# Two banks of an early convolution, and a gate, inside the last Mamba chunk's scan

## The chip, the cores and the metric

The kernel runs on one core of one Trainium2 chip. The metric is the device time of one execution in microseconds (us). A core has five instruction queues that run beside one another and wait for each other through semaphores: TensorE (PE: matmuls, with its weight loads shown apart as PEld), VectorE (DVE), ScalarE (ACT), GpSimd (POOL), and SyncE (SP), which here only starts DMA transfers. Each queue runs its instructions in the order in which they stand.

## What is computed

The reference is a network of four layers on an input of 2 x 256 x 32 x 32, all in float32. Only the first two matter here.

```python
# layer 0: two Mamba blocks, tokens = 1024 per image, 512 inner channels, 16 states
xr = u @ in_w + in_b;  xs, res = jnp.split(xr, 2, axis=-1)
xs = silu(causal_conv4(xs));  delta = softplus(dt @ dt_w + dt_b)
hst = exp(delta * A) * hst + delta * Bm * xs        # per state, a recurrence over tokens
y = einsum('bdn,bn->bd', hst, C) + xs * Dp
out = (y * silu(res)) @ out_w + out_b               # then layernorm, and added to the input
# layer 1: a dilated 7 x 7 convolution to 128 channels, a 1 x 1 convolution to 49 logits per
# pixel, a softmax over them, and with it a weighted sum of the 49 shifted images
k = conv(conv(x, w1, dilation=2, padding=6) + b1, w2) + b2;  attn = softmax(k, axis=1)
x = einsum('bkchw,bkhw->bchw', shifts, attn)
...
```

`silu(res)` is the gate. Layers 2 and 3 (linear attention, softmax attention, two mixtures of experts) take the second half of the time and are the same in both kernels.

## The kernel before, in words

**Chunks.** Layer 0 (`layer0`, L575) works on 2,048 tokens in four chunks of 512 for each of two blocks, eight units in all. `front` (L293) makes a chunk's inputs, `scan` (L415) runs the recurrence, `back` (L485) turns its sum into the chunk's result and adds it to `x`.

**The scan.** For each of 16 states, a DMA on SP brings a row of B to all partitions; POOL multiplies it with `du` (L461, two products of 128 x 1024 into `h`, six buffers, which are three states); ACT makes the decay (L468, four times, into PSUM buffers `da`); DVE runs the recurrence (L472, four scans of 128 x 512). The generator `rest` (L434) then turns the state's result: four times, PE transposes four 128 x 128 blocks into a PSUM tile `ht` (L440, three buffers), and DVE adds the tile, scaled, to `ya` (L449). For states 0 and 10 ACT does that (L447).

**PSUM.** It holds eight banks. In the last unit they are two for `da` (`m_da2`, L634), one for the convolution (`m_acc`, L635), two for `mm` and three for `ht`.

**The early convolution.** Layer 1's two convolutions are folded into one set of weights in advance (`taps`). `Taps.convolve` (L748) computes the logits of one image into up to three PSUM banks of 16 rows x 32 columns. Its 56 steps are four weight groups u (3, 0, 1, 2) by seven taps by two halves of the channels; a step issues one matmul for each bank that it was given and that the tap reaches:

```python
for k, a in acc.items():
    lo, hi = max(16 * k, r0), min(16 * k + 16, r0 + W)
    if lo < hi:
        nc.tensor.matmul(a[:, lo - 16 * k : hi - 16 * k, co : co + n], lhsT=lhsT, ...)   # L762
    yield
```

Bank 0 is reached over 16, 10, 12 and 14 rows by the four groups, bank 1 over 16 rows by each, and bank 2 over 6, 4 and 2 rows by the last three; a tap's width is 32, 26, 28, 30, 30, 28 or 26 columns. So bank 0 has 56 matmuls over 20,800 columns, bank 1 56 over 25,600, bank 2 42 over 4,800. A float32 matmul leaves two records in the trace; a transpose leaves one. `Taps.read` (L770) copies a finished bank to `lg`: half of it by ACT (L781), then half by DVE (L779). The weights lie in `early_3`, `early_0`, `early_1`, `early_2`, loaded by SP (L740) into buffers that earlier chunks have left free.

**The order.** `scan` has 63 slots, one after each recurrence on DVE but the first; `paced` (L552) spreads side work over them by (steps, how many, first slot, last slot). In the last unit that is the ninth to sixteenth step of the previous chunk's `back`, and bank 0 of the first image in slots 3 to 63. After the scan, the last transposes are issued, and `both` (L566) issues three steps of the convolution of banks 1 and 2 to one step of the last chunk's `back`. The program's order is a priority: when the instructions are placed, one that has no buffer yet lets later ones pass, so the order on each engine differs from the listing.

**`back` by steps.** Four gate groups (PE L494, two matmuls; ACT L498) and one Silu over all (L502); four `y` (PE L507, L512; DVE L516 multiplies by the gate); four `out` (PE L524, L528); the normalization (DVE L160 to L166, ACT L150, L168); two times four transposes (L179), ACT L540, and POOL's two additions to `x` (L543, L548).

**Layer 1.** It loads the same weights again as `pair` (memset by POOL, L737, DMA by SP, L740) into memory that `early` held, transposes image 0 for the weighted sum (`xk`: copies by POOL L856, PE L857, ACT L861), and convolves the second image (`acc`, L762), whose last 512 tokens are what the last chunk's `back` writes.

Of the kernel before, what the change touches and what calls it, by code (L numbers as in the profile page):

```python
# [10 lines left out]
F32 = mybir.dt.float32  # L11
# [8 lines left out]
P = 128  # L20
# [7 lines left out]
TC = 512  # L28
# [523 lines left out]
def paced(n, parts):  # L552

    taken = [0] * len(parts)
    for slot in range(n):
        for i, (steps, many, first, end) in enumerate(parts):
            while taken[i] < many and slot >= first + (end - first) * taken[i] / many:
                next(steps, None)
                taken[i] += 1
        yield  # L560
    for steps, *_ in parts:
        for _ in steps:
            pass


def both(a, b, n):  # L566

    for i, _ in enumerate(a):
        if i % n == n - 1:
            next(b, None)  # L570
    for _ in b:
        pass


def layer0(net, x, x_dram, m1, m2, load_image, taps, conv_dram, lg):  # L575

    tc, nc = net.tc, net.nc  # L580
    with (
        tc.tile_pool(name="m_w", bufs=1) as wpool,
        tc.tile_pool(name="m_one", bufs=1) as one,
        tc.tile_pool(name="m_two", bufs=2) as two,
        tc.tile_pool(name="m_scan", bufs=2) as scanp,
        tc.tile_pool(name="m_dram", bufs=2, space=DRAM) as dram,
        tc.tile_pool(name="m_mm", bufs=2, space=PSUM) as ps_mm,
        tc.tile_pool(name="m_ht", bufs=3, space=PSUM) as ps_ht,
        ExitStack() as last,
    ):  # L590
        ps_da = last.enter_context(tc.tile_pool(name="m_da", bufs=3, space=PSUM))
        xt = x.rearrange("p c b t -> p c (b t)")
        pools = (wpool, one, two, scanp, dram, ps_mm, ps_da, ps_ht)
        blocks = [
            Mamba(net, "m1", pools, xt, None, *m1), Mamba(net, "m2", pools, xt, x_dram, *m2)
        ]
        norm = GroupNorm(net, wpool, ps_ht, x)
        blocks[0].load()
        for _ in blocks[0].diagonals():
            pass  # L600
        load_image()
        for _ in blocks[0].load_rest():
            pass
        rows = net.first_rows(wpool, ["m1_out_b", "m2_out_b"])
        for m, r in zip(blocks, rows):
            m.out_b = r
        norm.image(0)
        units = [(m, j) for m in blocks for j in range(NCH)]
        norm.image(1)
        for _ in units[0][0].front(0, alone=True):  # L610
            pass
        before, done = iter(()), []
        aside = taps.make(ps_mm, conv_dram)
        for u, (m, j) in enumerate(units):
            steps = [(b, Mamba.GATED, 0, 35) for b in done]
            fronts = []
            for a, k in units[u + 1 : u + 2]:
                if k == 0:
                    a.load()
                fronts.append(a.front(k))  # L620
            if u == NCH - 2:

                steps.append((blocks[1].diagonals(), NDC * 4, 26, 38))
            rest = m.load_rest() if u and j == 0 else iter(())
            steps += [(f, Mamba.HEAD, 0, 38) for f in fronts]
            steps += [(rest, 1, 37, 38)]
            steps += [(f, 16, 38, 62) for f in fronts] + [(b, 7, 40, 61) for b in done]
            steps += [(rest, 1, 62, 63)]
            if u + 1 < len(units):
                n = 9 if u else 12  # L630
                steps += [(islice(aside, n), n, 40, 63)]
            else:
                last.close()
                m.ps_da = last.enter_context(tc.tile_pool(name="m_da2", bufs=2, space=PSUM))  # L634
                ps_acc = last.enter_context(tc.tile_pool(name="m_acc", bufs=1, space=PSUM))  # L635

                def place(u):
                    pool, tag, w = {
                        3: (one, "pre", TC + 3), 0: (two, "xs", TC), 1: (two, "delta", TC),
                        2: (two, "du", TC),  # L640
                    }[u]
                    a = pool.tile(
                        [P, NDC, w], F32, tag=tag, name=f"early_{u}",
                        bufs=3 if tag == "xs" else None,
                    )
                    return taps.load(u, a.rearrange("p d t -> p (d t)"))

                pair = {u: place(u) for u in taps.ORDER}
                acc = {0: taps.bank(ps_acc.tile([P, TC], F32, tag="acc", name="early_acc"))}
                steps += [(taps.convolve(0, pair, acc), 56, 3, 63)]  # L650
            before = m.scan(j, before, paced(63, steps), u == 0)
            done = [m.back(j)]
        taps.read(acc, lg)
        for _ in before:
            pass
        acc = {
            k: taps.bank(ps_ht.tile([P, TC], F32, tag="ht", name=f"early_acc{k}")) for k in (1, 2)
        }
        both(taps.convolve(0, pair, acc), done[0], 3)
        taps.read(acc, lg)  # L660

# [944 lines left out]
def conv_attn_hybrid(ctx: ExitStack, tc: tile.TileContext, a: dict, out: bass.AP):  # L1606
# [6 lines left out]
    with tc.tile_pool(name="conv_w", bufs=2) as convw:  # L1613
        def load_x(b):
            for cc in range(NCC):
                nc.sync.dma_start(x[:, cc, b, :], a["x"][b, cc])

        load_x(0)
        taps = Taps(net, convw, main, x, a["l1_w1"], a["l1_w2"])
        layer0(  # L1620
            net, x, a["x"],
            [a[f"m1_{k}"] for k in ("in_w", "out_w", "xproj_w", "dt_w")],
            [a[f"m2_{k}"] for k in ("in_w", "out_w", "xproj_w", "dt_w")],
            lambda: load_x(1), taps, conv_dram, lg,
        )
# [117 lines left out]
```

## Time and profile before

| what | value |
|---|---|
| time, median of 3 runs (lowest, highest) | 2186.85 us (2185.29, 2189.43) |
| the profiled execution's own time | 2188.29 us |
| its span in the trace | 2186.6 us |
| mean TensorE clock granted | 0.918 |
| busy: PE / DVE / ACT / POOL | 87% / 64% / 44% / 47% of the span |
| last chunk's first recurrence starts | 913.8 us |
| last chunk's last transposes start | 1033.7 us |
| first matmul of the second image's convolution starts | 1116.6 us |

A view of groups gives a line of the kernel, engine, operation, the tile written and the tiles read, how often, busy time, mean duration, and the idle time of the engine just before, with what ended it. The timeline gives start, length, engine and line in order of time. A view of windows gives, for a stretch of time, each engine's busy time with the number of its records in brackets, and the mean granted clock (PEclk). Matmuls are pipelined: a record's length is longer than the distance to the next, so the pace of PE is read from distances between starts.

### The profile page before, as it was taken

How to read it: one execution, taken by the hardware profiler on the slowest of the kernel's cores; microseconds unless marked ns; L12 is line 12 of the kernel's file. 1: busy time of each engine (PE TensorE's matmuls, PEld its weight loads, DVE VectorE, ACT ScalarE, POOL GpSimd, SP SyncE). 2: the span in 40 equal slices, each digit the busy share in tenths (PEclk: the TensorE clock that was granted, in tenths of full speed). 3: DMA queues.
4: the chain of work that ended last, by engine and by line, in shares of the span. 5: the costliest groups of instructions: out<-in, count | busy, mean ns of one | idle time of the engine just before them, and what ended most of it. 6: DMA issues, size and time to landing. Idle time of an engine off the chain costs nothing.

```text
span 2186.6 us, 27311 instructions
## 1 busy us (share of the span) xinstructions
PE 1894.0 (87%) x9652; PEld 1335.5 (61%) x9652; DVE 1400.3 (64%) x2210; ACT 959.2 (44%) x1610; POOL 1028.9 (47%) x726
## 2 busy tenths in 40 slices
PE   6888898898978888788999989949999599859996
PEld 2464555556555655454646556539999467649995
DVE  6999998999999999899005475752222544432223
ACT  4676677767777767645013454411111132301111
POOL 3796787959698686965025420012332000023331
PEclk9869889898989889899999999969999799979997
DMA  2121121111212111310030100028998200059997
GB/s 106 45 68 39 37 69 35 58 35 45 62 47 60 38 49 35 85 42 17 0 64 1 48 15 10 20 82 306 326 329 323 82 10 10 20 206 327 329 323 292
DMA packets 90499, 223.87 MB, mean 102 GB/s; under 512 B 35467, under 2 KB 51728, under 8 KB 79732
## 3 DMA queue, kind: packets, MB, share of 16 engines
q1 hardware_dynamic: 77636, 198.29, 27.1%
q0 software_dynamic: 7728, 19.15, 2.9%
q10 hardware_dynamic: 4992, 4.59, 0.7%
q8 instruction: 81, 1.33, 0.3%
q14 instruction: 62, 0.51, 0.1%
HBM read 204.60 MB, written 19.37 MB: 102 GB/s over the span
## 4 chain that ended last, share of the span: by engine, by line
PE 32%; DVE 22%; issue 19%; POOL 11%; ACT 10%; DMA 5%; POOLq 0%; SPq 0%; DVEq 0%; ACTq 0%
DVE m_h L472 11%; DVE m_ya L449 6%; PE acc L762 3%; POOL x L1520 3%; POOL l_yd L1570 3%; PE m_ht L440 3%; PE early_acc L762 3%; PE av L1276 3%; ACT m_da L468 2%; PE sc L1250 2%; DMA l_yd<-y,target 2%; POOL m_h L461 2%; PE h L1099 2%; PE m_xd_ps L351 1%; PE w L1108 1%
## 5 line engine op out<-in xcount | busy, mean ns | idle before, releaser
L461 POOL TENSOR_TENSOR m_h<-m_du,m_b 128x1024 f32<-128x1024 f32 x254 | 594.5, 2364 | 196.0 <-PE m_ht L440 95.8
L440 PE MATMUL m_ht<-ident,m_h 128*128 128x128 f32 x2048 | 361.2, 305 | 119.4 <-DVE m_ya L449 83.9
L440 PEld LDWEIGHTS m_ht<-ident,m_h 128*128 128x128 f32 x2048 | 259.5, 154 | 317.8 <-DVE m_ya L449 112.7
L468 ACT ACTIVATE m_da<-m_delta,m_aneg 128x512 f32<-128x512 f32 x512 | 349.5, 690 | 220.8 <-DVE m_h L472 220.1
L1520 POOL DMA_INDIRECT x<-l_zd,source x82 | 84.8, 1034 | 573.1 <-DVE source L1465 217.1
L449 DVE SCALAR_TENSOR_TENSOR m_ya<-m_ht,m_ct,m_ya 128x512 f32<-128x512 f32 x448 | 320.2, 733 | 18.4 <-PE m_ht L440 17.5
L472 DVE TENSOR_TENSOR_SCAN m_h<-m_da,m_state,m_h 128x512 f32<-128x512 f32 x256 | 318.7, 1271 | 14.7 <-POOL m_h L461 8.7
L472 DVE TENSOR_TENSOR_SCAN m_h<-m_da,m_h 128x512 f32<-128x512 f32 x256 | 303.3, 1210 | 23.6 <-ACT m_da L468 13.1
L1550 PEld LDWEIGHTS h<-xts,we 128*128 128x128 f32 x2528 | 298.4, 194 | 7.1 <-issue 3.4
L1550 PE MATMUL h<-xts,we 128*128 128x128 f32 x2528 | 299.4, 277 | 2.2 <-issue 1.7
L1557 DVE TENSOR_TENSOR hid<-hid,h 128x512 f32<-128x512 f32 x79 | 54.3, 688 | 258.9 <-PE h L1550 258.9
L1556 ACT ACTIVATE hid<-h 128x512 f32<-128x512 f32 x79 | 47.2, 598 | 384.6 <-issue 324.0
L1564 PE MATMUL o<-we,hid 128*128 128x256 f32 x632 | 150.4, 380 | 2.2 <-DVE y L1569 1.6
L1570 POOL DMA_INDIRECT l_yd<-y,target x79 | 79.3, 1003 | 142.6 <-DVE y L1569 136.3
L1564 PEld LDWEIGHTS o<-we,hid 128*128 128x128 f32 x632 | 113.7, 190 | 15.7 <-DVE y L1569 2.8
L336 PE MATMUL m_conv<-m_pre,m_taps 128*128 128x512 f32 x240 | 114.6, 596 | 6.7 <-ACT m_gate L498 5.6
L762 PE MATMUL early_acc<-x,early 128*98 128x448 f32 (+21 forms) x308 | 97.0, 447 | 0.0
L762 PE MATMUL acc<-x,pair 128*98 128x416 f32 (+21 forms) x308 | 93.6, 452 | 0.0
L1569 DVE COPY y<-o 128x256 f32<-128x256 f32 x79 | 33.6, 425 | 69.6 <-PE o L1564 69.6
L309 PE MATMUL m_in<-x,m_in_sb 128*128 128x512 f32 x128 | 68.8, 663 | 9.8 <-ACT m_pre L313 6.9
L762 PEld LDWEIGHTS acc<-x,pair 128*98 128x98 f32 x308 | 47.7, 167 | 39.9 <-issue 34.5
L528 PE MATMUL m_out<-m_out_sb,m_xs 128*128 128x256 f32 x256 | 68.7, 397 | 0.0
(318 smaller groups left out, 2843.3 us busy)
## 6 DMA issues: line engine op xcount, KB each, us to landing
we<-in_l_experts_dram SPq DMA_DIRECT2D x82, 1536.0 KB
m_b<-m_bd SPq DMA_DIRECT2D x128, 256.0 KB
w<-in_l_w_dram SPq DMA_DIRECT2D x21, 256.0 KB
l_zd<-l_z SPq DMA_DIRECT2D x7, 512.0 KB
l_yl<-l_yd SPq DMA_DIRECT2D x10, 256.0 KB
l_yl<-l_yd ACTq DMA_DIRECT2D x10, 256.0 KB
early<-taps SPq DMA_DIRECT2D x7, 343.0 KB
pair<-taps SPq DMA_DIRECT2D x7, 343.0 KB
```

The costliest lines, as they stand in the source:

```text
L309: nc.tensor.matmul(ps, lhsT=self.in_sb[:, kc, mc * P : (mc + 1) * P], rhs=self.xt[:, kc, tok], start=(kc == 0), stop=(kc == NCC - 1),)
L336: nc.tensor.matmul(ps, lhsT=self.taps[:, dc * 4 + k, :], rhs=pre[:, dc, k : k + TC], start=(k == 0), stop=(k == 3),)
L440: nc.tensor.transpose(ps[:, dc * P : (dc + 1) * P], hs[dc // G][:, dc % G, i * P : (i + 1) * P], net.ident,)
L449: nc.vector.scalar_tensor_tensor(ya[:, i, :], ps, c, ya[:, i, :], ALU.mult, ALU.add)
L461: (nc.vector if start and n == 0 else nc.gpsimd).tensor_mul(h, du[:, g * G : (g + 1) * G, :], b.unsqueeze(1).to_broadcast(half))
L468: nc.scalar.activation(da, delta[:, dc, :], AF.Exp, scale=self.aneg[:, i : i + 1])
L472: nc.vector.tensor_tensor_scan(h, da, h, 0.0 if first else state[:, n, dc : dc + 1], ALU.mult, ALU.add)
L762: nc.tensor.matmul(a[:, lo - 16 * k : hi - 16 * k, co : co + n], lhsT=lhsT, rhs=self.x[:, kc, b, lo - r0 : hi - r0, ci : ci + n], start=(u ...
L1520: nc.gpsimd.indirect_dma_start(out=x, out_offset=None, in_=zd[:, :], in_offset=bass.IndirectOffsetOnAxis(ap=source[:, g : g + 1], axis=0), ...
L1550: nc.tensor.matmul(ps[:, at], lhsT=w12[:, s, kc, at], rhs=xt[:, kc * P : (kc + 1) * P], start=(kc == 0), stop=(kc == NCC - 1),)
L1564: nc.tensor.matmul(ps[:, :C], lhsT=ht[:, mc * P : (mc + 1) * P], rhs=w[:, 8 + mc, :], start=(mc == 0), stop=(mc == NHC - 1),)
L1570: nc.gpsimd.indirect_dma_start(out=yd[g], out_offset=bass.IndirectOffsetOnAxis(ap=target[:, g : g + 1], axis=0), in_=y, in_offset=None, bo ...
```

## The change

Bank 1 of the first image follows bank 0 in the last scan, in the same PSUM bank, with a read of each when it is done; the last chunk's own gate (five steps of `back`) is placed in slots 44 to 58; after the scan only bank 2 and the other eleven steps of `back` are left. Lines below the edit move down by seven.

```diff
                 pair = {u: place(u) for u in taps.ORDER}
-                acc = {0: taps.bank(ps_acc.tile([P, TC], F32, tag="acc", name="early_acc"))}
-                steps += [(taps.convolve(0, pair, acc), 56, 3, 63)]
+                def early():
+                    for k in range(2):
+                        a = ps_acc.tile([P, TC], F32, tag="acc", name=f"early_acc{k}")
+                        acc = {k: taps.bank(a)}
+                        yield from taps.convolve(0, pair, acc)
+                        taps.read(acc, lg)
+
+                steps += [(early(), 112, 3, 63)]
+            own = m.back(j)
+            if u + 1 == len(units):
+
+                steps += [(islice(own, 5), 5, 44, 58)]
             before = m.scan(j, before, paced(63, steps), u == 0)
-            done = [m.back(j)]
-        taps.read(acc, lg)
+            done = [own]
         for _ in before:
             pass
-        acc = {
-            k: taps.bank(ps_ht.tile([P, TC], F32, tag="ht", name=f"early_acc{k}")) for k in (1, 2)
-        }
+        acc = {2: taps.bank(ps_ht.tile([P, TC], F32, tag="ht", name="early_acc2"))}
         both(taps.convolve(0, pair, acc), done[0], 3)
         taps.read(acc, lg)
```

## The prediction

> **What bounds the kernel now.** I first asked where the work that the change touches lies. The view of windows, over the last chunk's scan and what follows it (start and end in us, length, then busy time and records of PE, PEld, DVE, ACT and POOL, the clock and the DMA share):
>
> ```profile
> core 0: us, PE busy (x) PEld busy (x) DVE busy (x) ACT busy (x) POOL busy (x), PEclk, DMA share, GB/s
> ...
> 934.50:985.00 50.50, 44.20 (x242) 29.00 (x243) 50.50 (x58) 22.61 (x30) 32.88 (x15) 1.00 0.14 42
> 985.00:1034.60 49.60, 43.56 (x207) 25.13 (x206) 49.17 (x63) 27.38 (x41) 28.39 (x14) 1.00 0.06 16
> 1034.60:1060.00 25.40, 25.40 (x99) 14.21 (x98) 1.86 (x3) 5.17 (x5) 0.00 (x0) 1.00 0.00 1
> ...
> 1110.30:1116.60 6.30, 4.49 (x14) 2.17 (x15) 0.71 (x2) 2.69 (x8) 4.07 (x13) 0.73 0.97 159
> ```
>
> In the scan DVE is busy all the time. After it DVE is empty and PE is full, until 1110.3, and then neither is. So the stretch has two limits, one after the other, and moving PE's work from the second into the first can only gain as much as PE has free in the scan. How much that is, the busy column doesn't tell, since matmuls overlap; PE's own timeline does, by distances between starts:
>
> ```profile
> 949.36 0.66 PE L440 MATMUL m_ht<-ident,m_h 128*128 128x128 f32 x4
> 949.85 0.63 PE L762 MATMUL early_acc<-x,early 128*98 128x280 f32 x2
> 950.32 1.02 PE L507 MATMUL m_y<-m_xs,m_skip 128*128 128x512 f32 x2
> ...
> 953.03 0.66 PE L440 MATMUL m_ht<-ident,m_h 128*128 128x128 f32 x4 [0.73 <-DVE m_ya L449]
> ...
> 1033.72 1.04 PE L440 MATMUL m_ht<-ident,m_h 128*128 128x128 f32 x8
> 1034.59 9.50 PE L762 MATMUL early_acc<-x,early 128*98 128x512 f32 x24
> 1043.93 1.88 PE L494 MATMUL m_g<-x,m_gate_sb 128*128 128x512 f32 x4
> 1045.65 0.86 PE L762 MATMUL early_acc<-x,early 128*98 128x416 f32 x2
> ```
>
> Four transposes take 0.44 (eight from 1033.72 to 1034.59) to 0.49 us (949.36 to 949.85); I use 0.47. The 24 records at 1034.59 cover 5,568 columns twice in 9.34 us: 0.84 ns per column and record. A gate group takes 1.72 (1043.93 to 1045.65). From the same timeline, a `y` group takes 2.65 and an `out` step 2.45. At 953.03 PE stood idle because DVE had not freed an `ht` buffer: that is the scan's usual wait. DVE's pace, from its timeline, is 1.19 for a recurrence and 0.64 for an addition to `ya`, 1.83 for both:
>
> ```profile
> 988.27 1.28 DVE L472 TENSOR_TENSOR_SCAN m_h<-m_da,m_state,m_h 128x512 f32<-128x512 f32 x1
> 989.46 0.74 DVE L449 SCALAR_TENSOR_TENSOR m_ya<-m_ht,m_ct,m_ya 128x512 f32<-128x512 f32 x1
> 990.10 1.28 DVE L472 TENSOR_TENSOR_SCAN m_h<-m_da,m_state,m_h 128x512 f32<-128x512 f32 x1
> ```
>
> Last, what starts layer 1, in the timeline of POOL and PE:
>
> ```profile
> 1105.02 1.27 POOL L548 TENSOR_TENSOR x<-x,m_x 128x512 f32<-128x512 f32 x1
> ...
> 1110.26 0.68 POOL L737 MEMSET pair<- 128x686 f32 x1 [2.59 <-PE early_acc L762]
> ```
> ```profile
> 1111.42 0.41 PE L857 MATMUL xk<-ident,xs 128*128 128x128 f32 x2 [1.22 <-POOL pair L737]
> ...
> 1116.57 13.93 PE L762 MATMUL acc<-x,pair 128*98 128x512 f32 x31
> ```
>
> The last chunk was in `x` at 1106.3, but the weights' memory came free only with the last early matmul, at 1110.2; DMA and 13 `xk` transposes then took until 1116.57. That start is the point I price.
>
> **What the Trainium skill says.** "Perfetto Trace Analysis", Identifying the Most-Contended Engine: matmul busy time is a poor measure of how full PE is. The trace agrees: transposes of 273 ns each start 0.11 us apart. "TensorE: Matmul & The Clock Gate", Part 1: an idle window of about 3.4 us drops the array to half clock. It agrees: the clock is 1.00 up to 1110.3 and 0.73 in the thin 6.3 us after it. "ScalarE: Activation LUTs", What ACT_TABLE_LOAD costs: about 1,283 ns a load; the rows before and after the gate's Silu show 1283 each.
>
> **The change, part by part.** Times are those of the profiled execution (2188.29 us, span 2186.6), 1.4 above the median.
>
> *PE's work in the scan.* Both orders agree up to state 1's transposes, at 925.2. From there to the end of bank 1 PE has: the other 50 matmuls of bank 0, 18,048 columns x 2 x 0.835 ns = 30.1; bank 1, 25,600 x 2 x 0.835 = 42.8 (new); transposes of states 1 to 14, 56 x 0.47 = 26.3; the previous chunk's four `y`, 10.6, four `out`, 9.8, and last 1.5 gate groups, 2.6; its own four gates, 6.9 (three of them lay in the scan's end already); eight result transposes, 0.9. Sum 130.0, so bank 1 can't end before 1055.2, where bank 0 ended at 1023.7 and the last transposes at 1034.6. PE, not DVE, is the scan's limit now.
>
> *PE's idle time in it.* I followed the order in which the changed program's instructions stand, with the paces above. First half: by the end of bank 0 PE needs 55.7, to 980.9, and DVE, which has 24 recurrences, 21 additions and 3 gate products from 934.55 to the addition that frees the buffer for state 7's third tile, needs 43.9, to 978.5. So PE is just ahead as the limit; it waits 1.4 for state 1's recurrence, 2.1 for one buffer behind three recurrences, 0.8 for another: 4.3. POOL's product for a state needs the buffers of three states earlier, freed by PE; it is ready at the moment it is needed (979.2 for 978.5), no more.
>
> *The wait that is added.* Bank 1 uses bank 0's buffer. Its first matmul waits for both reads; DVE's stands behind 4 recurrences and 3 additions. PE has two and a half tiles of transposes to do meanwhile, and all later transposes are queued behind: 0.8 us.
>
> *The gate.* Its matmuls need `mm` buffers, which the previous chunk's `out` holds until the normalization has read it on ACT; that waits for DVE, which waits for a transpose. The second gate group so stops PE by about 2.4 us (bounds 0 and 6). On ACT the Silu and two table loads (1.91 + 2 x 1.28) now stand ahead of the last two decays; DVE has over 10 us of slack there, so I cost them at nothing; without the slack they would cost 4.5. In the tail, before, Silu lay beside the convolution: removing it gains nothing there by itself. No part that is moved issues a DMA; SP's queue keeps its order.
>
> Bank 1 ends at 1055.2 + 4.3 + 0.8 + 2.4 = 1062.7; call that E.
>
> *The tail.* DVE reads bank 1 behind ACT (1.0), then adds four tiles (2.6): E + 3.7. Four `y`, with the first half done: E + 12.2; gate product, then `out` with bank 2 between, E + 24.8; bank 2's middle, 44 records at 0.11 to 0.17 us each (no row shows it alone; I take 0.12), covers the normalization's 4.1: E + 30; transposes, E + 31.6; two ACT results, then POOL's four additions, 1.27 each, the last perhaps late for its DMA (0.8): E + 38. In the new order POOL's memset and band work (2.1) follow, then `xk`; nine transposes now precede `acc`, not 13, and take 3.3: E + 43.7 = 1106.4. The DMA (6.2 after the last early matmul, E + 33) is hidden. What is late last is POOL's chain, no longer PE.
>
> *Sum.* 1116.57 - 1106.4 = 10.2. Four transposes fall into `acc` (0.4), and the thin stretch is 10 us instead of 6, which can lengthen the half clock: 0 to 3, I take 1. Gain about 9; 2186.85 - 9 = 2177.5.
>
> **The rivals.** (1) *The scan keeps its idle time.* In the scan before, PE's own waits at transposes are
>
> ```profile
> PE m_ht L440 <- DVE m_ya L449: 13.4, 21, 2.6
> ```
>
> plus what weight loads hide; from 925.2 to 1034.6 PE works about 87 of 109 (the sum above without bank 1, with state 15's transposes and three of its own gates), idle 22. If tile by tile PE goes on waiting for DVE, with 22 idle instead of 7.5, bank 1 ends at 1077.2 and layer 1 starts at 1120.9: 4.3 later and the 1.4 of the sum, 5.7 us slower, 2192.6. It is slower from 16.5 us of idle on. Against it: in the new order DVE's recurrences stand one to two states ahead of the additions, so after state 8 DVE owes PE nothing for 13 us. (2) *The gain is eaten* by waits of ACT, POOL and the clock at their upper bounds (gate +3.6, bank 2 +3, clock +2): 2186, within 0.2%, which is about what a measurement of this kernel can tell from no change. (3) *PE runs full.* With no idle at all and no clock loss the gain is 17: 2170. (4) *Bank 1 doesn't fit in the scan.* Excluded: its first matmul stands among state 8's transposes, its last ahead of state 15's.
>
> **How the numbers follow.** The forecast, a gain of 4.4 to 14, 0.56; (3), more than 14, 0.14; (2) 0.18; (1) 0.12. Faster 0.70, same 0.18, slower 0.12. The forecast's own range is 2172 to 2182; 2167 to 2190 takes in (2), nearly all of (3) and the milder half of (1).
>
> **What would show it.** Right: DVE no longer full after about 990, PE waiting little; bank 1's end near 1063; the last transposes near 1065 instead of 1034; then some 41 us to the first `acc`, ending in POOL additions. Wrong: idle PE of more than 16.5 us between 925 and bank 1's end, waits on `m_ya`, or a half clock inside the scan.

## The result and the profile after

The changed kernel takes 2177.32 us (median of six runs, 2172.59 to 2179.29), the kernel before 2186.07 (six runs beside them, 2184.43 to 2189.43). The ratio is 0.9957, with a 95% interval of 0.9943 to 0.9970: faster by 0.43%, between 6.6 and 12.5 us, where a gain of about 9 (2177.5) had been forecast. Run a second time, unedited, it took 2175.75, ratio 0.9950 (0.9931 to 0.9969). The ratios are those on record with their intervals, and need not be the quotient of the two medians, which is 0.9960 here.

The profiled execution is the fastest of the six (2172.59 us, span 2170.9), and its span is 15.7 us shorter than that of before. Not all of this is the change. Split at two marks, the last chunk's first recurrence on DVE and the first matmul of the second image's convolution, the traces say:

| from the trace | before | after | after, second time |
|---|---|---|---|
| first recurrence of the last chunk at | 913.76 | 912.47 | 913.34 |
| from there to the last state's last four transposes | 120.40 | 151.31 | 151.27 |
| from the first recurrence to layer 1's first `acc` matmul ("the stretch") | 202.81 | 192.47 | 192.48 |
| `acc`, first to last matmul | 107.6 | 108.1 | 108.5 |
| what follows | 962.4 | 957.9 | 961.7 |

The stretch is 10.3 us shorter, and it repeats to 0.01 us. What lies ahead of it and behind it moves by several us from one execution to the next without any edit there, so I compare kernels by the stretch first, and by their medians second. (In the kernel before, the last four transposes end a row of eight that starts at 1033.72, so they start 0.44 later than that row.)

Three views answer to those shown of before. The windows of the changed kernel (start and end, length, then busy time and records of PE, PEld, DVE, ACT and POOL, the clock, the DMA share), over the scan to bank 1's end and the thin stretch after the tail:

```profile
core 0: us, PE busy (x) PEld busy (x) DVE busy (x) ACT busy (x) POOL busy (x), PEclk, DMA share, GB/s
933.20:983.70 50.50, 47.16 (x249) 31.98 (x248) 48.90 (x54) 23.73 (x32) 28.21 (x13) 1.00 0.13 37
983.70:1033.30 49.60, 49.05 (x198) 28.15 (x196) 35.60 (x46) 19.09 (x28) 23.34 (x10) 1.00 0.05 16
1033.30:1061.60 28.30, 26.54 (x102) 14.24 (x103) 15.71 (x19) 13.07 (x17) 9.71 (x6) 1.00 0.03 10
...
1094.30:1104.90 10.60, 3.08 (x9) 1.68 (x10) 1.83 (x11) 1.97 (x6) 8.76 (x17) 0.69 0.57 109
```

In the first 50 us DVE is still nearly full, as before. In the second 50 us it is busy for 35.6 of 49.6, and PE has taken its place with 49.05. PE's timeline in the scan shows where it still stands (the idle time before a row is in square brackets):

```profile
944.33 0.66 PE L440 MATMUL m_ht<-ident,m_h 128*128 128x128 f32 x4 [1.55 <-DVE m_ya L449]
...
960.71 0.66 PE L440 MATMUL m_ht<-ident,m_h 128*128 128x128 f32 x4 [1.07 <-DVE m_ya L449]
...
986.36 0.44 PE L440 MATMUL m_ht<-ident,m_h 128*128 128x128 f32 x2 [0.25 <-DVE m_ya L449]
986.75 3.36 PE L769 MATMUL early_acc<-x,early 128*98 128x512 f32 x8
...
1035.06 3.70 PE L494 MATMUL m_g<-x,m_gate_sb 128*128 128x512 f32 x8 [2.06 <-ACT m_o L168]
...
1061.61 0.60 PE L440 MATMUL m_ht<-ident,m_h 128*128 128x128 f32 x4
```

Bank 1's first matmul stands at 986.75, its last just ahead of the transposes at 1061.61, which is E. On the axis of before, 1.29 later, that is 1062.9. And the tail's end, POOL's timeline, then PE's:

```profile
1093.97 2.48 POOL L543 TENSOR_TENSOR x<-x,m_r 128x512 f32<-128x512 f32 x2 [5.14 <-ACT m_r L540]
1096.41 1.26 POOL L548 TENSOR_TENSOR x<-x,m_x 128x512 f32<-128x512 f32 x1
1097.99 1.26 POOL L548 TENSOR_TENSOR x<-x,m_x 128x512 f32<-128x512 f32 x1 [0.32 <-DMA m_x<-in_x_dram]
1099.31 0.68 POOL L744 MEMSET pair<- 128x686 f32 x1
1099.92 0.90 POOL L852 MEMSET band<- 128x384 f32 x2
```
```profile
1093.30 0.99 PE L769 MATMUL early_acc<-x,early 128*98 128x60 f32 x10
1101.12 0.71 PE L864 MATMUL xk<-ident,xs 128*128 128x128 f32 x2 [6.83 <-POOL xs L863]
...
1104.94 17.61 PE L769 MATMUL acc<-x,pair 128*98 128x512 f32 x40
```

PE is done with the first image at 1094.2 and then waits 6.8 us, for POOL: the last additions, the memsets and the first copy. In the kernel before it was POOL that waited for PE here.

### The profile page after: what moved, and what is told of

Same layout as the page of the kernel before. It is cut to its first block, busy times and chain, and to the rows that moved or that the text cites. A ratio compares the mean times of both kernels' runs of the same rounds, so it can differ in the third digit from the quotient of the medians.

```text
span 2170.9 us, 27318 instructions
## 1 busy us (share of the span) xinstructions
PE 1889.3 (87%) x9652; PEld 1345.8 (62%) x9652; DVE 1402.7 (65%) x2210; ACT 959.9 (44%) x1611; POOL 1027.6 (47%) x726
## 4 chain that ended last, share of the span: by engine, by line
PE 32%; DVE 22%; issue 19%; POOL 12%; ACT 9%; DMA 5%; POOLq 0%; SPq 0%; ACTq 0%; DVEq 0%
DVE m_h L472 11%; DVE m_ya L449 5%; PE acc L769 3%; POOL x L1527 3%; POOL l_yd L1577 3%; PE m_ht L440 3%; PE av L1283 3%; POOL m_h L461 3%; PE early_acc L769 2%; PE sc L1257 2%; ACT m_da L468 2%; DMA l_yd<-y,target 2%; PE h L1106 2%; PE w L1115 1%; PE m_xd_ps L351 1%
## 5 line engine op out<-in xcount | busy, mean ns | idle before, releaser
L440 PEld LDWEIGHTS m_ht<-ident,m_h 128*128 128x128 f32 x2048 | 266.2, 156 | 299.0 <-issue 105.2
L1571 PEld LDWEIGHTS o<-we,hid 128*128 128x128 f32 x632 | 113.7, 190 | 15.7 <-DVE y L1576 2.8
L769 PE MATMUL early_acc<-x,early 128*98 128x448 f32 (+24 forms) x308 | 100.5, 453 | 0.0
L494 PE MATMUL m_g<-x,m_gate_sb 128*128 128x512 f32 x128 | 66.5, 633 | 3.9 <-ACT m_o L168 2.1
```

Source lines behind the costliest of these rows:

```text
L440: nc.tensor.transpose(ps[:, dc * P : (dc + 1) * P], hs[dc // G][:, dc % G, i * P : (i + 1) * P], net.ident,)
L1571: nc.tensor.matmul(ps[:, :C], lhsT=ht[:, mc * P : (mc + 1) * P], rhs=w[:, 8 + mc, :], start=(mc == 0), stop=(mc == NHC - 1),)
```

## The experiments

My theory: the gain is idle PE time in the scan that bank 1 fills, PE is the scan's limit from there on, and the tail ends in POOL's chain. Rivals: the gate and its Silu leaving the tail bring the gain; or the loop of POOL's product, DVE's recurrence and the `ht` buffers still sets the scan's length. All edits are to the changed kernel. "Stretch" is as above (192.48 for the changed kernel); times are medians. The runs come in four sets, each with runs of the kernel before beside it (medians 2185.58 to 2186.61), so across sets the ratio is the better measure. A stretch is read from one execution.

| kernel | median (lowest, highest) | ratio to before (95%) | last transposes | stretch |
|---|---|---|---|---|
| `bank1_alone` | 2175.51 (2170.51, 2181.95) | 0.9954 (0.9935, 0.9972) | 142.06 | 193.04 |
| `gate_alone` | 2183.90 (2180.50, 2194.72) | 0.9997 (0.9985, 1.0009) | 122.64 | 201.37 |
| `x_on_dve` | 2174.12 (2167.51, 2179.74) | 0.9950 (0.9933, 0.9967) | 151.34 | 191.26 |
| `gate_early` | 2171.93 (2169.59, 2172.91) | 0.9937 (0.9923, 0.9951) | 148.89 | 190.02 |
| `after_again` | 2175.75 (2173.02, 2181.11) | 0.9950 (0.9931, 0.9969) | 151.27 | 192.48 |
| `bank1_half` | 2180.86 (2174.72, 2184.40) | 0.9968 (0.9955, 0.9982) | 133.09 | 174.28 |
| `three_banks` | 2181.70 (2175.68, 2188.68) | 0.9975 (0.9964, 0.9986) | 164.57 | 200.58 |
| `x_dve_four` | 2169.12 (2166.86, 2170.64) | 0.9915 (0.9899, 0.9930) | 152.91 | 191.54 |
| `combo` | 2171.05 (2168.57, 2175.86) | 0.9932 (0.9913, 0.9951) | 148.90 | 187.51 |
| `combo_band` | 2170.14 (2165.85, 2174.80) | 0.9922 (0.9902, 0.9943) | 148.92 | 189.37 |
| `dense` | 2176.02 (2172.67, 2181.99) | 0.9956 (0.9942, 0.9970) | 151.92 | 192.57 |
| `weights_first` | 2173.78 (2166.89, 2180.15) | 0.9947 (0.9928, 0.9967) | 148.90 | 186.39 |

**The two parts apart.** First bank 1 in the scan, with the gate left behind:

```diff
-                steps += [(islice(own, 5), 5, 44, 58)]
+                pass
```

> Bank 1 in the scan, but the last chunk's own gate left to the sixteen steps after it. My theory (PE has the same work wherever the gate stands, and PE is the limit): the wait of 2.1 us for the mm buffers goes, bank 1 ends about 9 us earlier (6.9 of gates and 2.1 of wait) and the tail is 7 to 11 us longer, since five of bank 2's steps fewer are left to cover the normalization (some 1.5 us) and Silu stands ahead of the gate products: 2177 to 2180, most of the gain kept. The rival (the gate and its Silu leaving the tail is what brings the gain): 2183 to 2186, near the kernel before.

Bank 1 ended 139.9 us after the first recurrence, 9.3 earlier than with the gate in the scan (149.1), and the tail from there to layer 1 was 53.2 us for 43.3. The stretch is 0.6 longer than with both parts and 9.8 shorter than before. The median is 1.5 below the range that I gave, which the spread of the runs covers. So bank 1 alone brings nearly all.

The other half, the gate in the scan and bank 0 alone beside it:

```diff
-                    for k in range(2):
+                    for k in range(1):
...
-                steps += [(early(), 112, 3, 63)]
+                steps += [(early(), 56, 3, 63)]
...
-        acc = {2: taps.bank(ps_ht.tile([P, TC], F32, tag="ht", name="early_acc2"))}
+        acc = {
+            k: taps.bank(ps_ht.tile([P, TC], F32, tag="ht", name=f"early_acc{k}")) for k in (1, 2)
+        }
```

> The own gate in the scan, but bank 0 alone beside it; banks 1 and 2 after the scan as in the kernel before. My theory (the gain is PE's idle time in the scan that bank 1 fills, and DVE stays the limit of this scan): only one to one and a half gate groups really change place, 1.7 to 2.6 us, so 2183.5 to 2185, a gain of about 2. The rival (Silu and its table loads leaving the tail are the gain): a gain of 5 or more, 2177 to 2181.

The stretch is 1.4 us shorter than before, a little under my 1.7; the ratio can't tell it from no change. The rival that Silu leaving the tail is the gain has fallen: it asked for 5 or more.

**Is PE the limit in the scan?** Half of bank 1 left out:

```diff
-                        yield from taps.convolve(0, pair, acc)
+                        for _ in taps.convolve(0, pair, acc, range(NCC - k)):
+                            yield
+                            if k:
+                                yield
...
-    def convolve(self, b, pair, acc):
+    def convolve(self, b, pair, acc, kcs=range(NCC)):
...
-                for kc in range(NCC):
+                for kc in kcs:
...
-                                stop=(u == 2 and v == 6 and kc == NCC - 1),
+                                stop=(u == 2 and v == 6 and kc == kcs[-1]),
```

> The changed kernel, with the half of bank 1's matmuls that read the second 128 input channels left out (the logits of these rows are not the reference's); the other half stays in its slots, 43 to 63 included. It leaves out 12,800 columns of PE, 21.4 us at 0.84 ns per column and record. My theory (PE is what the scan's second half waits for): bank 1 ends 18 to 21 us earlier, with PE's idle time up by 0 to 3 because DVE's own limit, some 132 us after the first recurrence, is near; median 2156 to 2160. The rival (the loop of POOL's products, DVE's recurrences and the three ht buffers sets the scan's length, and bank 1 rides partly for nothing): less than 14 us, 2163 or more.

The stretch is 18.2 us shorter for 21.4 us of matmuls left out, as the theory has it. Even this understates it: in this trace the gate groups ran partly at half clock,

```profile
1029.01 7.11 PE L494 MATMUL m_g<-x,m_gate_sb 128*128 128x512 f32 x12 [2.42 <-ACT m_o L168]
```

12 records, three groups, in 6.95 us (to the transposes at 1035.96) where three take 5.2 by the forecast's pace, 1.8 lost. So some 20 of 21.4 us came straight off the end, and the loop of POOL, DVE and `ht` doesn't set the length. My forecast of the median fell, though: 2180.86. Of the trace, the part after `acc` is 24 us longer than in the changed kernel, and nearly all of that lies in its last quarter, from 811 us after layer 1's first matmul on (282 us for 259 in `after_again`, 1,754 PE records for 1,628). Other logits give the last layer's mixture of experts other data, and its work depends on them; that this is the cause I only argue, but it isn't in the stretch. The median of this run says nothing on the change.

From the other side, more work in the scan:

```diff
-                    for k in range(2):
+                    for k in range(3):
...
-                steps += [(early(), 112, 3, 63)]
+                steps += [(early(), 168, 3, 63)]
...
-        acc = {2: taps.bank(ps_ht.tile([P, TC], F32, tag="ht", name="early_acc2"))}
-        both(taps.convolve(0, pair, acc), done[0], 3)
-        taps.read(acc, lg)
+        for _ in done[0]:
+            pass
```

> Bank 2 in the last scan too (168 steps in slots 3 to 63, the same PSUM bank a third time), and after the scan only the eleven steps of back. My theory (PE has no free time left in the scan, and bank 2 in the tail lay for nothing beside the normalization): the scan ends 8.6 us later for bank 2's 84 records at 0.10 each, and up to 8 more since DVE's recurrences of the last states then have little PE work beside them; the tail gets shorter by some 4.5 only (3 of bank 2 between the out steps, 1.5 after them): 2181 to 2189, slower than the changed kernel by 4 to 12. The rival (the scan still has idle PE time to fill, or the weights' transfer, which now could start earlier, is late last): 2173 to 2177.

The stretch is 8.1 longer, inside the 4 to 12. The last transposes come 13.3 later, where bank 2's own work is 8.6, and the rest is 5.2 shorter. Up to 1.7 of the 13.3 is half clock behind a wait of 2.58 us at the gate groups (clock 0.50 from 1055.1 to 1058.5). PE's timeline shows both prices, the wait at an earlier bank change and the uncovered normalization:

```profile
971.93 1.10 PE L768 MATMUL early_acc<-x,early 128*98 128x512 f32 x2 [3.22 <-DVE lg L785]
...
1099.48 2.24 PE L179 MATMUL mm_t<-ident,m_o 128*128 128x128 f32 x8 [3.06 <-ACT m_o L168]
```

In the changed kernel bank 2's middle stands in the second place and the transposes have no wait. So what idle time PE has left in the scan is none that bank 2 could fill, and bank 2 is better where it is.

**What PE still waits for in the scan.** The gate ahead of the previous chunk's `out`:

```diff
-                steps += [(islice(own, 5), 5, 44, 58)]
+                steps += [(islice(own, 5), 5, 38, 42)]
```

> The changed kernel with the own gate's five steps in slots 38 to 42, ahead of the previous chunk's out, in place of 44 to 58. My theory (two gate groups stop PE for 2.1 us because the mm buffers are held until the normalization has read them, and PE is the limit): the wait goes, bank 1 ends 1.5 to 2.5 us earlier, 2175 to 2176. The rival (PE isn't the limit there; or Silu with its two table loads, 4.5 us on ACT, now stops the decays while DVE needs them): bank 1 ends at the same time or up to 2 us later, 2177 to 2179.

> The changed kernel once more, unedited, so that it stands on the same chip and beside the same runs as the other three. Expected 2177 (2175 to 2179), and from the last chunk's first recurrence to layer 1's first matmul of the second image 192.5 us, as in its first trace.

The second run of the changed kernel came out as expected, 192.48 and 2175.75. With the early gate the wait of 2.06 on ACT's `m_o` is gone from PE's timeline, bank 1 ends and the last transposes come 2.4 earlier, inside my 1.5 to 2.5, and the stretch is 2.5 shorter. The median is below my range by 3 us, more than the stretch explains. It is 3.8 below that of the changed kernel's second run, and its runs lie closer together (3.3 us for 8.1), though the intervals of the two ratios overlap.

Then the waits of the first half, by packing the matmuls more densely (with the early gate):

```diff
-                steps += [(early(), 112, 3, 63)]
+                steps += [(early(), 112, 3, 57)]
```

> The early gate, and the 112 steps of banks 0 and 1 spread over slots 3 to 57 in place of 3 to 63. My theory (what is left between the sum of PE's work and bank 1's end are PE's waits in the first half, about 4.8 us in four or five pieces, where DVE is still as late as PE): with more matmuls to each slot PE falls behind sooner, the waits get smaller by 1 to 3 us, and layer 1 starts 187 to 189 us after the first recurrence (190.0 with the early gate alone). The rival (the last slots, with no matmuls beside them, make PE wait for DVE again, as with three banks): 190 to 193.

Here the theory's forecast fell: 192.57, 2.6 longer than `gate_early` and inside the rival's range. Bank 1's last matmul started 1.2 earlier than in `gate_early`, but the last transposes 3.0 later. PE's timeline says why:

```profile
947.64 0.88 PE L440 MATMUL m_ht<-ident,m_h 128*128 128x128 f32 x4 [2.40 <-DVE m_ya L449]
...
986.83 2.66 PE L769 MATMUL early_acc<-x,early 128*98 128x512 f32 x6 [2.25 <-DVE lg L786]
...
1062.64 0.66 PE L440 MATMUL m_ht<-ident,m_h 128*128 128x128 f32 x4 [0.40 <-DVE m_ya L449]
```

The longest wait didn't shrink (2.40 where it was 2.19), and 3.4 us at half clock followed it, in place of two waits of 0.51 and 1.07; the bank change came at a moment when DVE's read stood behind two recurrences that waited for POOL, 2.25 where it was 0.26, and at the end transposes were left without matmuls between them, though the wait that the rival foresaw there is only 0.40. What a bank change costs is a matter of its place.

**What is late last in the tail.** The four additions on DVE:

```diff
-            nc.gpsimd.tensor_add(xt[:, cc, tok], xt[:, cc, tok], r)
+            adder = nc.vector if m == "m2" and j == NCH - 1 else nc.gpsimd
+            adder.tensor_add(xt[:, cc, tok], xt[:, cc, tok], r)
...
-                nc.gpsimd.tensor_add(xt[:, cc, tok], xt[:, cc, tok], x)
+                adder.tensor_add(xt[:, cc, tok], xt[:, cc, tok], x)
```

> The changed kernel with the last chunk's four additions to x on DVE, which is idle there, in place of POOL. My theory (POOL's chain of four additions of 1.27 us, then memset, band and copies, is late last in the tail): DVE needs some 0.6 us for each, POOL's memset and copies no longer stand behind them, and layer 1 starts 2.5 to 4 us earlier: 2173.5 to 2175, about 3 below the changed kernel. The rival (the transfer of the weights, 6.2 us after the last early matmul, or the normalization is late anyway): no change, 2177.

The stretch is 1.2 us shorter: neither my 2.5 to 4 nor the rival's nothing. That the median, 2174.12, falls into my range all the same is chance. DVE's timeline has the next thing in line:

```profile
1093.62 0.69 DVE L549 TENSOR_TENSOR x<-x,m_x 128x512 f32<-128x512 f32 x1 [1.08 <-DMA m_x<-in_x_dram]
```

The second piece of the input can only be loaded when the first addition has freed its buffer. So the pieces went elsewhere:

```diff
-                x = self.one.tile([P, TC], F32, tag="r", name=f"{m}_x_{j}_{cc}", bufs=3)
+                if j < NCH - 1:
+                    x = self.one.tile([P, TC], F32, tag="r", name=f"{m}_x_{j}_{cc}", bufs=3)
+                else:
+                    if cc == 0:
+                        late = self.one.tile([P, NDC, TC], F32, tag="gate", name=f"{m}_x_{j}")
+                    x = late[:, cc, :]
```

> As the run with the four additions on DVE, and the last chunk's two pieces of the input are loaded into the gate's memory, free after the gate products, in place of the third and a reused piece buffer, so that both transfers land ahead of the normalization. In the trace of the run with the additions on DVE alone, DVE stood 1.1 us for the second piece, whose buffer came free only with the first addition, and layer 1's weights were sent for only when the last addition was done. My theory (additions, then the weights' transfer or the xk transposes, 5.7 us, then layer 1): the additions end 1.3 to 1.5 us earlier and layer 1 starts as much earlier, 189.8 us after the first recurrence, median about 2173. The rival (the last early matmul or its read on ACT and DVE then is late last): less than 0.7.

The tail did what was forecast: from the last transposes to layer 1 it took 38.6 us, where `x_on_dve` took 39.9 and the changed kernel 41.2. The stretch didn't, 191.54 for 189.8, because this execution lost 1.6 us in the scan, at the same instructions in the same order. PE's timeline and the windows of `x_dve_four`, and then PE's timeline of `after_again`:

```profile
1032.75 5.38 PE L494 MATMUL m_g<-x,m_gate_sb 128*128 128x512 f32 x8 [2.06 <-ACT m_o L168]
```
```profile
1032.70:1036.00 3.30, 3.25 (x4) 1.51 (x5) 2.06 (x3) 2.10 (x4) 0.00 (x0) 0.51 0.00 0
```
```profile
1035.89 3.70 PE L494 MATMUL m_g<-x,m_gate_sb 128*128 128x512 f32 x8 [2.06 <-ACT m_o L168]
```

The same wait of 2.06 us halved the clock behind it in the one and not in the other; the last section shows what decides that. The median, 2169.12, lies some 4 us below my forecast although this stretch is longer: the profiled execution is the slowest of the six, and whether the other five lost the 1.6 us too is not shown. The early gate takes that wait away, so both edits were put together:

> Gate early (slots 38 to 42), the four additions on DVE, and the two pieces of the input in the gate's memory, together. My theory (the first shortens the scan, the others the tail after it, so they add up): from the last chunk's first recurrence to layer 1 the run with the early gate took 190.0 us; the tail from the last chunk's first y to layer 1 was 2.5 us shorter with the other two edits than without (39.5 for 42.0); so 187.5, and a median of about 2169.5. The rival (with the gate early, Silu or the y groups hold up something else in the tail): 189 or more.

The stretch is 187.51, as forecast: 5.0 below the changed kernel, 15.3 below the kernel before. The median, 2171.05, is 1.5 above the forecast, and the ratio, 0.9932, is not below the 0.9915 of `x_dve_four`; so what the early gate adds to the other two edits is shown by the traces alone.

Two runs were to say which of the chains ahead of layer 1 is late last. The band's memsets moved to DVE:

```diff
-            nc.gpsimd.memset(a.rearrange("p r c h -> p (r c h)"), 0.0)
+            nc.vector.memset(a.rearrange("p r c h -> p (r c h)"), 0.0)
```

> The same combination, with the two memsets of the band on DVE in place of POOL, where they stand between the weights' memset and the first xk copy and take 0.84 us. It tells the two chains apart that end together ahead of layer 1: if POOL's copies and PE's xk transposes are late last, as I predicted, layer 1 starts 0.8 us earlier than in the combination (186.7 us after the first recurrence); if the transfer of the weights, which is issued when the last addition is done, is late last, it starts at the same time (187.5, within 0.2).

Neither number came: 189.37. The first transpose did start 0.8 earlier (182.9 for 183.7), but in this program's order 15 `xk` transposes stand ahead of `acc`, not nine, in PE's timeline:

```profile
1098.10 6.69 PE L870 MATMUL xk<-ident,xs 128*128 128x128 f32 x15 [3.46 <-POOL xs L869]
```

At 0.43 each, the six more cost 2.6. That an edit to a memset moves the order of transposes makes it no clean test. The other one forced the order:

```diff
+                    if b == 0 and q == 0:
+                        nc.gpsimd.tensor_copy(xs[:, 0, 0, :1], pair[3][:, 0, :1])
                     nc.gpsimd.tensor_copy(xs, x6[:, cc, b, q // 4, r : r + 4])
```

> The combination, and one column of layer 1's first weights is copied by POOL into the first xk piece before the piece itself, so that the xk transposes stand behind the second image's first matmuls on PE. It takes the nine xk transposes (4.1 us from the first of them to the first matmul in the combination) away from ahead of layer 1; what is then late last is the transfer of the weights, issued when the last addition is done. In the combination's trace the transfer's data begin to flow 2 us after its issue, at some 240 GB/s, 343 KB: it should land about 3.5 to 4 us after the issue. My theory (POOL's copies and the xk transposes were late last, the transfer hidden): the first matmul starts 1.5 to 2 us earlier, 185.5 to 186 us after the first recurrence, and about half of it is given back, since the transposes then stand inside the convolution: 2169 to 2170.5. The rival (the transfer lands only as late as the transposes end, 5.6 us after its issue): 187.3 or later, 2171.

SP's timeline has the issues, the first of them that of the first weights, and POOL's has the copy that waits for these:

```profile
1088.13 10.88 SPq L753 DMA_DIRECT2D pair<-taps  x7
```
```profile
1092.45 0.30 POOL L870 COPY xs<-pair 128x1 f32<-128x1 f32 x2 [2.72 <-DMA pair<-taps]
```

The weights are there 4.3 us after the issue (1088.13 to 1092.45), a little later than my 3.5 to 4, and layer 1 starts 186.39 after the first recurrence, 1.1 earlier than in `combo`: there the transfer was not late last, POOL's copies and the transposes were, by 1.1 us. Here the transfer is. The gain is less than my 1.5 to 2, and the median, 2173.78, lies 3.3 above my range. Nearly all of it is given back: the end of `acc` comes only 0.2 earlier, since the nine transposes, 0.11 each at full clock, now stand inside it.

The smallest stretch that isn't given back inside `acc` is that of `combo`; by medians `x_dve_four`, `combo_band`, `combo` and `gate_early` lie within 2.8 us, which these runs don't rank. All four are below both kernels.

## Why the prediction was right

**PE's work and pace.** Sum to bank 1's end 130.0, so 1055.2 at the earliest on the axis of before; measured E 1062.9, forecast 1062.7. (A slip in the sum at its end: 2186.85 less 9 is 2177.85, not 2177.5.)

**PE's idle time.** Here the total is right and its parts are not, so that it meets to 0.2 us is partly luck. Forecast 4.3 + 0.8 + 2.4 = 7.5; from state 1's transposes (923.9) to E the trace has 137.7 us for 130.0 of work, 7.7 lost. I find 3.3 of it in four waits for `ht` buffers in the first half (1.55, 0.51, 1.07, 0.20), 0.25 at the bank change and 2.06 at the gate. Where I had a wait of 1.4 for state 1's recurrence, PE ran at half clock from 924 to about 927.5 and so came too late to wait; that is some 1.7. The first half so lost 5.0, not 4.3. Nor is PE its limit, as I had it. Bank 1's first matmul stands 74.2 to 74.3 us after the first recurrence in all ten runs that keep its slots, though seven of them ran 3.4 us at half clock on the way, between 11 and 37 us after the first recurrence, and three (`gate_early`, `x_dve_four`, `weights_first`) none there. A loss of 1.7 us on PE that moves nothing shows that PE isn't what is late there; the waits that get shorter for it are those for DVE. PE is the limit from bank 1 on, where the same loss moves the end (`x_dve_four`, 1.6). The bank change was over-priced here, but `dense` (2.25) and `three_banks` (3.22) show that such a wait can be larger than I allowed.

**The gate.** The wait for `mm` buffers was real, and avoidable (`gate_early`). That Silu and its table loads cost nothing in the scan was right: with the early gate they stand among the decays, and the last transposes are only earlier.

**POOL's product.** "Ready at the moment it is needed, no more": DVE did wait for it, 15.0 us in all between 908 and 1063 by the view of waits (6.5 once). It cost next to nothing, because DVE owed PE nothing then, as `bank1_half` confirms.

**The tail.** Forecast E + 43.7, measured E + 43.3. Term by term: bank 2's middle starts at E + 25.5 (24.8); its 44 records take 0.102 each (0.12), so the transposes come at E + 30.0 (30); the additions end at E + 37.6 (38); the first transpose of `xk` 1.9 after that (2.1); nine of them take 3.8 (3.3).

**One reason in it was wrong.** I had the weights' transfer start after the last early matmul, at E + 33, and called it hidden by that. It is issued at 1099.27, when POOL's last addition is done, 5 us after the last early matmul; in the kernel before it was issued at 1110.34, behind the last early matmul, 4 us after the last addition. In both it comes behind the later of the two. Nor did it take the 6.2 us that I gave it, which in the kernel before is the time to `acc`, transposes included. It is hidden all the same, by some 1.3 us (4.3 from issue to landing in `weights_first`, 5.67 from issue to `acc` here). And so an edit to the additions moves the transfer and the copies together.

**After the start of layer 1.** I took off 0.4 for transposes and 1 for the half clock; `acc` is 0.5 and 0.9 longer in the two traces. In the median, 8.75 us against 10.3 in the stretch, less that.

**The rivals.** PE lost 7.7 us in the scan, not 22 (1) nor nothing (3). Waits at their upper bounds (2) didn't come; but half clock inside the scan is a loss that I hadn't priced. Two of my signs of being wrong did show, waits on `m_ya` (3.3 us) and a half clock inside the scan; both lie in the first half, where DVE is the limit, and the half clock moved nothing.

## What to carry to other kernels

Two stretches with different limits can be worth merging ("Perfetto Trace Analysis" of the Trainium skill, Optimization Strategy, suggests interleaving such regimes; here that brought 10.3 us for 42.8 us of matmuls moved), and the gain is at most the idle time of the engine that receives the work, which must be counted by distances between starts, minus what the receiving engine then waits for. Once it is full, more work moved there costs at least its whole length, and work that covered a latency elsewhere should stay. After such a move look again at what is late last at the end: here a chain of POOL additions, copies and transposes that had been covered, worth another 5 us together with one wait for buffers.

## What the runs showed of the hardware

"TensorE: Matmul & The Clock Gate" of the Trainium skill, Part 1, puts the drop to half clock after an idle window of about 3.4 us, and calls the window free-running. The traces agree on the half, on the length of a step and on the free running, not on the idle time that a drop takes. In each of the 14 traces, every stretch at half clock starts on a grid of 3.41 us and lasts a whole number of its steps (the last one is cut off by the end of the program), and the grid lies elsewhere in each execution. What a wait does depends on how it falls on the grid. These are the step with the wait of 2.06 us at the gate groups and the step behind it, by the windows of `x_dve_four` and then of `after_again`:

```profile
1029.32:1032.73 3.41, 1.36 (x7) 0.56 (x5) 3.41 (x6) 1.75 (x4) 1.36 (x1) 1.00 0.00 0
1032.74:1036.15 3.41, 3.40 (x4) 1.51 (x5) 2.02 (x3) 2.06 (x4) 0.00 (x0) 0.50 0.00 0
```
```profile
1031.70:1035.11 3.41, 2.13 (x9) 0.88 (x7) 3.41 (x6) 0.98 (x2) 2.13 (x1) 1.00 0.00 0
1035.12:1038.53 3.41, 2.64 (x6) 1.25 (x7) 2.67 (x3) 3.41 (x7) 0.00 (x0) 1.00 0.00 0
```

In `x_dve_four` the wait lies inside one step, which leaves PE 1.36 of 3.41 us, and the next step is at half clock. In `after_again` the grid cuts the wait in two, and the clock stays. From 3 us after the last chunk's first recurrence to its last transposes, the 14 traces have some 550 steps at full clock. Thirteen of them are followed by half clock: PE has no record in 1.77 to 2.57 us of these, and in at most 1.83 us of the others. So in these scans about half a step without PE was enough, in one piece or in several, and not a whole one. It explains why 1.54 us in one piece dropped the clock in the changed kernel's first trace (920.76 to 924.17, 1.77 without PE in all, then 0.50) and 1.53 at the same place didn't in `gate_early` (the grid cuts it at 920.25). The trace of before, which the forecast found in agreement with the page, says the same: the step ahead of its half clock (1109.76 to 1113.17) has PE records for 1.70 us.

What a drop costs depends on its place: nothing in the first half of the scan of the ten runs named above, where PE then waits less for DVE, and 1.6 us in the second, where PE is the limit.
